# Three edits of order in an attention and non-local block: one activation behind a copy, four position groups in another order, and the last image's folded weights in two parts

## The chip, the cores and the metric

The kernel runs on one core of a Trainium2 chip. The metric is the device time of one execution in microseconds (us), the median of several runs. Every number is of 32-bit floating point work.

## The reference

The input is x, 8 images of 512 channels and 32 x 32 = 1024 positions. Two layers follow each other.

```python
# layer 0: attention with 8 heads of 64 channels, softmax over keys m
q, k, v = Wq x + bq, Wk x + bk, Wv x + bv          # 1x1 convolutions, 512 -> 512
out = softmax(q^T k / sqrt(64)) v
x = x + Wp out + bp
# layer 1: non-local block with 256 inner channels, then batch norm
g, theta, phi = g_w x + g_b, theta_w x + theta_b, phi_w x + phi_b
f = theta phi^T / 1024                             # 256 x 256 for each image
z = W_w (f g) + W_b + x
out = gamma (z - mean(z)) / sqrt(var(z) + eps) + beta   # over images and positions, by channel
```

The mean and the variance of a channel need z of all eight images, so no output can leave before the last image's z of that channel is there.

## The kernel before

**Work and order.** One image follows another: q, k, v, the attention of 16 units, the projection by Wp (`project`), theta and phi (`theta_phi`), and g, f and z (`nonlocal_`). The order of TensorE's matmuls and of VectorE's adds is pinned by hand: every instruction that goes through `pe()` or `dve()` keeps its place relative to the others that do, and a scheduler places the remaining ones around them. SyncE issues the loads and stores. ScalarE (ACT) makes the exponentials and copies results out of PSUM, VectorE (DVE) adds, and GpSimd (POOL) adds too.

**Products with fewer multiplications.** A product of two matrices is split into 2 x 2 quarters and made from seven products of sums of quarters in place of eight. `seven` does that for one product. `data` holds the quarters of x and their sums (`"11"`, `"21"`, `"22"`, `"t1"` to `"t4"`), and every product goes into the PSUM bank that `SEVEN` names for it. With positions_out the positions stand on the partitions of the result: a product then consists of four groups `parts` of 128 positions each, i = 0 to 3, where two of them fill half a bank. With `inner="tp"` (theta and phi of images 1 to 7, called ptp) some of the seven are again made from smaller products (`nested`), woven in between. The first product of ptp is `"11"`: its moving data are the folded weights w_tp, and its weights (the stationary operand) are columns of x, 128 positions at a time. These columns of x are finished only just before, by the last adds of the projection on DVE (L504, `add_to`, in place in x): two adds for columns 256 to 511, then two for columns 0 to 255.

`six` makes q, k and v of images 1 to 7 with seven products at each of two levels. `plain` makes product "11" in two halves: two matmuls each, then ACT writes the result with the bias into two places, the temporary T6 and quarter 11 (`begin`, the activation in L568). Then come three pairs of products of 14 steps each, in this order:

```python
    ORDER = "0a 0b 1a 2a 2b 1b 5a 4a 5b 4b 3a 3b 6a 6b".split()
```

The digit names the product, the letter the member of the pair. Products 0 and 2 of one member add up in the same bank, so 2b adds to what 0b left there. After a step its readers take the bank's content: the first reader of a quarter is an ACT copy (L479), the others are DVE adds (L481); the quarters T6 and 11 are only added to. The matmuls of these steps have line L473 for q and k. Sums of input quarters that later steps need are made on DVE or POOL in between (L294).

**The end.** Images 5, 6 and 7 (`LATE = 3`) get their z only when all else is done, since their f and g wait. `wf` is f folded into W and divided by 1024: two parts of 128 x 512 for each image, made by TensorE (pwf, L959) and scaled by ACT (L960). `late_unit` makes z of one image and channel chunk oc (128 channels) from wf and g: four matmuls into one bank (pz, L1038), each with two records in the profile, one DVE operation that adds bias and x (L1043), and two `bn_stats` (L1046). Image 5's z of chunk 0 stands ahead of image 7's wf, in `before_wf`. Then `last_z` runs:

```python
        order = [B - LATE, B - 1, *range(B - LATE + 1, B - 1)]
        for oc in range(CC):
            images = order if oc else [B - 1]
            for b in images:
                for h0, h1 in ((0, 1), (1, 2)) if b == images[-1] else ((0, NH),):
                    late_unit(b, oc, h0, h1)
            finish(oc, *begin(oc))
```

`begin` gathers the statistics into mean and variance (mv, L1062) and takes the square root on ACT (gs, L1064); `finish` makes scale and shift with three small DVE operations (L1070 to L1072), scales eight images (ACT L1079; in the last chunk half of them DVE L1077), and writes each one out from SyncE (L1080).

Of the kernel before, what the change touches and what calls it, by code (L numbers as in the profile page):

```python
# [30 lines left out]
def unshifted(ctx: ExitStack, tc: tile.TileContext, a: dict, out: bass.AP):  # L31
# [30 lines left out]
    def pe(ins):  # L62
        tc.keep_in_program_order(ins)
# [289 lines left out]
    def seven(name, w, data, positions_out, first, add, between=None, early=False,  # L353
              by_chunk=False, inner=None, via=()):

        nk, half = w.shape[2], w.shape[3]
        tags = list(free)
        free[:] = [tags[3], tags[1], tags[0], tags[2]] if early else [tags[3], tags[1], tags[2], tags[0]]  # L360
        slots, begun = {}, set()
        steps, counts = iter(()), iter(())
        if inner:
            free[:] = [tags[0], tags[2], tags[1], tags[3]] if inner == "p" else [tags[1], tags[2], tags[3], tags[0]]
            products, goes_to, counts = INNER[inner]
            counts = iter(counts)
            steps = nested(name, w, data, tags[2:], first, add, goes_to, positions_out)
        else:
            products = LATER if early == "later" else EARLY if early else SEVEN

        def read(reads, ps):
            for to, is_first in reads:
                (first if is_first else add)(to, ps)

        for n, (what, wi, di, s, reads) in enumerate(products):
            if s not in slots or early and what == "t4" or inner == "p" and what == "s3t3":
                slots[s] = bank(tags[s], f"{name}_{s}_{n}")
                begun -= {one for one in begun if one[0] == s}
            ps, d = slots[s], data[di]
            if positions_out:  # L380
                parts = [(ps.rearrange("p h (i f) -> p (h i) f", f=half)[:, i, :], i * half // 512,
                          lambda k, i=i: d[:, k, i * P:(i + 1) * P], lambda k: w[:, wi, k, :])
                         for i in range(512 // P)]
            else:
                parts = [(ps[:, m, :], m, lambda k, m=m: w[:, wi, k, m * P:(m + 1) * P], lambda k: d[:, k, :])
                         for m in range(half // P)]
            work = [(*part, k) for part in parts for k in range(nk)]
            if by_chunk and what in ("11", "s1t1"):
                work.sort(key=lambda one: one[4])
            for i, (to_ps, at, lhsT, rhs, k) in enumerate(work):  # L390
                pe(nc.tensor.matmul(to_ps, lhsT(k), rhs(k), start=(s, at) not in begun, stop=(k == nk - 1),  # L391
                                    skip_group_check=True))
                begun.add((s, at))
                for _ in range(next(counts, 0)):
                    next(steps)
            if inner and what in via:
                via[what](reads, ps)
            else:
                read(reads, ps)
            if between and n in between:  # L400
                between[n]()
# [4 lines left out]
    def six(name, w, data, positions_out, at, begin, third, fills, by_scalar=False, later=None):  # L406

        fills = dict(fills)
        shape = [P, 4, 256] if positions_out else [P, 2, 512]
        temps = {}  # L410

# [15 lines left out]
        def plain():  # L427
            d = data["11"]
            for half in range(2):
                ps = next_bank(f"{name}_0_{half}")[:, 0, :]  # L430
                if positions_out:
                    ps = ps.rearrange("p (i f) -> p i f", f=256)
                for i in range(2 if positions_out else 1):
                    for k in range(2):
                        if positions_out:
                            at = (half * 2 + i) * P
                            pe(nc.tensor.matmul(ps[:, i, :], d[:, k, at:at + P], w[:, 0, k, :],  # L437
                                                start=(k == 0 and i == 0), stop=(k == 1), skip_group_check=True))
                        else:
                            pe(nc.tensor.matmul(ps, w[:, 0, k, half * P:(half + 1) * P], d[:, k, :],  # L440
                                                start=(k == 0), stop=(k == 1), skip_group_check=True))
                for q in ("T6", "11"):
                    at_ = to(q)[:, half * 2:half * 2 + 2, :] if positions_out else to(q)[:, half, :]
                    begin(at_, ps, half)
            load_w("first")

        plain()
# [2 lines left out]
        for n, pair in enumerate(SIX):  # L450
            if n == 2:
                add("12", "22")
                add("12", "T6")
                for one in fills.pop("middle", ()):
                    one()
            slots = [next_bank(f"{name}_in_{n}_{i}") for i in range(4)]
            free[:] = [free[2], free[3], free[0], free[1]]
            begun = set()
            for step, which in enumerate(ORDER):
                _, wi, di, chain, reads = SEVEN[int(which[0])]  # L460
                m = "ab".index(which[1])
                outer, of, q = pair[m]
                a, d = w.inner(outer)[wi], data[f"inner {of}"][di]
                ps = slots[m if not chain else 2 + m][:, chain // 2, :256]
                start = (m, chain) not in begun
                begun.add((m, chain))
                if positions_out:
                    ps = ps.rearrange("p (i f) -> p i f", f=P)
                    for i in range(2):
                        pe(nc.tensor.matmul(ps[:, i, :], d[:, i * P:(i + 1) * P], a, start=start and not i, stop=True,  # L470
                                            skip_group_check=True))
                else:
                    pe(nc.tensor.matmul(ps, a, d, start=start, stop=True, skip_group_check=True))  # L473
                for (i, j), is_first in reads:
                    i, j = int(i) - 1, int(j) - 1
                    if is_first and q == "T7":
                        third(piece(q, i, j), ps, piece("T6", i, j), i)
                    elif is_first and q not in ("11", "T6"):
                        nc.scalar.copy(piece(q, i, j), ps)  # L479
                    else:  # L480
                        dve(nc.vector.tensor_tensor(piece(q, i, j), piece(q, i, j), ps, ALU.add))  # L481
                for one in fills.pop((n, step), ()):
                    one()
            load_w()
# [77 lines left out]
    def heads_of(b, what, w, bias, data, pin=lambda ins: None, steps=None, fills=None, **how):  # L562
# [2 lines left out]

        if fills is not None:
            def begin(to, ps, i):
                nc.scalar.activation(to, ps, AF.Identity, bias=bias[:, i:i + 1])  # L568

            def third(to, ps, of, i):  # L570
                if what == "q":
                    nc.scalar.activation(to, ps, AF.Identity, bias=steps[:, i:i + 1])
                else:
                    dve(nc.vector.scalar_tensor_tensor(to, ps, steps[:, i:i + 1], of, ALU.add, ALU.add))

            six(f"p{what}_{b}", w, data, False, lambda q: t[:, rows(q), cols(q)], begin, third, fills,
                what == "q", how.get("later"))
            return t
# [348 lines left out]
    def nonlocal_(b, xt, data, f, wg, before_wf, between=None, sums=None):  # L927
# [23 lines left out]
              between or {4: f_meanwhile}, early=bool(between))  # L951
        f = fs[0]

        before_wf()
        wf = block(f"wf_{b}")
        for d in range(IC):
            ps = next_bank(f"pwf_{b}_{d}")[:, 0, :]
            for c in range(IC):
# [90 lines left out]
            return sums  # L1049
        sums()  # L1050

    def last_z():
        order = [B - LATE, B - 1, *range(B - LATE + 1, B - 1)]
        for oc in range(CC):
            images = order if oc else [B - 1]
            for b in images:
                for h0, h1 in ((0, 1), (1, 2)) if b == images[-1] else ((0, NH),):
                    late_unit(b, oc, h0, h1)
            finish(oc, *begin(oc))

    def begin(oc):
# [51 lines left out]
    for b in range(B):  # L1113
# [137 lines left out]

        def before_wf():
            if last:
                late_unit(B - LATE, 0)
                z[b] = [xt[:, cc, :] for cc in range(CC)]
                reload(4, mats, "o")
                take_back(B - LATE + 1)
# [5 lines left out]
        if b == B - 2:  # L1263
            held.update(x=xt, both=both)
        else:
            nonlocal_(b, xt, data, None, weights("WgT"), before_wf, sums=both)
            load_w()
            if b in spill_g:
                put_away(b)
# [3 lines left out]
    dens, sane = both[:, 0, :], both[:, 1, :]  # L1273
    for to, d in own:
        nc.sync.dma_start(dens[:, to], d)
    last_z()


    good = const.tile([P, 1], F32, tag="good", name="good")
# [218 lines left out]
```

## Time and profile before

| | us |
|---|---|
| median of 3 runs | 2102.07 (2102.05 to 2102.19) |
| the profiled execution | 2102.2 |
| its span, first to last instruction | 2100.4 |
| TensorE busy in the span | 2076.9 (99%) |
| VectorE, ScalarE, GpSimd busy | 1442.6, 803.0, 818.3 |
| waits that ended last: TensorE's share of the chain | 98% |

The profile covers one execution; the 1.8 us between its time and its span lie ahead of the first and behind the last instruction. PE is the matmul stream of TensorE, and PEld its loading of stationary operands, which overlaps the matmuls. In a timeline each line has the start, the time to the end of the last record in the group, the engine, the line, the operation with output and inputs, and the number of records. A bracket gives the idle time of that engine just before, and what ended it. Each fp32 matmul appears twice, so four matmuls show as x8. Records of matmuls that follow each other closely overlap: their length is longer than the distance between two starts.

### The profile page before, as it was taken

What the parts mean: (1) busy time and instruction counts of PE and PEld (TensorE: products, weight loads), DVE (VectorE), ACT (ScalarE), POOL (GpSimd) and SP (SyncE); (2) the same over time, 40 slices, a digit from 0 to 9 for tenths busy, and PEclk for the clock granted to TensorE, in tenths of its full rate; (3) what the DMA queues carried; (4) which work ended last, traced back from release to release, by engine and by line L of the source; (5) the groups of instructions that cost most, each with busy time, mean ns of one, the idle gap of its engine ahead of it and who ended that gap; (6) DMA issues with size and microseconds to landing.
All of it is one profiled execution on the core that took longest, in us unless ns stands there. A gap on an engine that the chain in (4) does not pass through costs nothing.

```text
span 2100.4 us, 34471 instructions
## 1 busy us (share of the span) xinstructions
PE 2076.9 (99%) x13682; PEld 1176.0 (56%) x13682; DVE 1442.6 (69%) x2192; ACT 803.0 (38%) x1071; POOL 818.3 (39%) x689
## 2 busy tenths in 40 slices
PE   9999999999999999999999999999999999999995
PEld 4535864358733677336773377633876348743472
DVE  5587668775678656876567765677665775676756
ACT  1465204652046420564205641066312653056106
POOL 0024900448413583134922358223681338711010
PEclk9999999999999999999999999999999999999998
DMA  6254634445343443435324363153644345322668
GB/s 230 83 145 78 184 116 153 46 89 154 106 116 39 100 141 103 119 40 116 133 90 123 40 146 121 69 126 40 157 142 164 38 47 180 99 31 39 218 253 322
DMA packets 79697, 248.71 MB, mean 118 GB/s; under 512 B 17316, under 2 KB 25768, under 8 KB 77480
## 3 DMA queue, kind: packets, MB, share of 16 engines
q1 hardware_dynamic: 65656, 220.07, 32.3%
q0 software_dynamic: 12016, 24.80, 12.2%
q8 instruction: 110, 1.80, 0.4%
q10 hardware_dynamic: 1856, 1.56, 0.3%
q14 instruction: 59, 0.48, 0.1%
HBM read 164.64 MB, written 48.17 MB: 101 GB/s over the span
## 4 chain that ended last, share of the span: by engine, by line
PE 98%; ACT 1%; DVE 1%; DMA 0%; issue 0%
PE ps L638 21%; PE po L664 21%; PE ptp L391 7%; PE pv_in L470 6%; PE pp L391 6%; PE pk_in L473 6%; PE pq_in L473 6%; PE pg L391 5%; PE pz L391 3%; PE pp_in_s L342 3%; PE pf L916 2%; PE ptp_in_s L339 2%; PE pwf L959 1%; PE pv L437 1%; PE pq L440 1%; PE pq L391 1%
## 5 line engine op out<-in xcount | busy, mean ns | idle before, releaser
L641 ACT ACTIVATE e<-ps 128x1024 f32<-128x1024 f32 x512 | 523.0, 1025 | 412.0 <-PE ps L638 400.5
L694 POOL DMA_DIRECT2D fold<-acc x336 | 257.1, 816 | 921.7 <-DMA fold<-acc 543.3
L647 DVE TENSOR_TENSOR acc<-acc,e 128x1024 f32<-128x1024 f32 x384 | 469.9, 1224 | 93.2 <-ACT e L641 82.2
L638 PE MATMUL ps<-q,k 64*64 64x512 f32 x4096 | 529.2, 589 | 0.0
L664 PE MATMUL po<-e,v 64*64 64x512 f32 x4096 | 528.7, 589 | 0.0
L664 PEld LDWEIGHTS po<-e,v 64*64 64x64 f32 x4096 | 156.6, 133 | 282.9 <-issue 275.4
L638 PEld LDWEIGHTS ps<-q,k 64*64 64x64 f32 x4096 | 155.5, 133 | 283.2 <-issue 275.3
L947 ACT ACTIVATE g<-pg,gb 128x512 f32<-128x512 f32 x31 | 21.3, 688 | 366.5 <-PE pg L391 366.4
L645 DVE TENSOR_TENSOR acc<-e,e 128x1024 f32<-128x1024 f32 x64 | 78.3, 1224 | 114.5 <-ACT e L641 112.2
L391 PE MATMUL pp<-t_o,w_WpT 128*128 128x512 f32 x208 | 102.0, 592 | 0.0
L391 PE MATMUL ptp<-w_tp,t_x 128*128 128x256 f32 x400 | 96.1, 379 | 0.0
L756 POOL TENSOR_TENSOR o<-o,r 128x1024 f32<-128x1024 f32 x28 | 65.5, 2361 | 31.8 <-DMA r<-den_d 31.5
L391 PEld LDWEIGHTS ptp<-w_tp,t_x 128*128 128x128 f32 x400 | 72.3, 190 | 7.8
L821 POOL TENSOR_TENSOR x<-x,read 128x1024 f32<-128x1024 f32 x30 | 69.8, 2353 | 13.0 <-ACT read L818 13.0
L481 DVE TENSOR_TENSOR k<-k,pk_in 128x256 f32<-128x256 f32 x112 | 46.8, 421 | 39.5 <-PE pk_in L473 35.0
L391 PE MATMUL ptp<-w_tp,x 128*128 128x256 f32 x272 | 70.0, 381 | 0.8
L479 ACT COPY v<-pv_in 128x256 f32<-128x256 f32 x84 | 31.4, 374 | 95.0 <-DVE T_pv L481 25.5
L479 ACT COPY k<-pk_in 128x256 f32<-128x256 f32 x84 | 31.3, 372 | 92.0 <-PE pk_in L473 90.3
L481 DVE TENSOR_TENSOR v<-v,pv_in 128x256 f32<-128x256 f32 x112 | 46.3, 421 | 29.3 <-PE pv_in L470 22.8
L470 PE MATMUL pv_in<-w_WvT,i_t_x 128*128 128x128 f32 x448 | 59.2, 275 | 0.0
L473 PE MATMUL pk_in<-i_t_x,w_WkT 128*128 128x256 f32 x224 | 58.1, 381 | 0.1
L473 PE MATMUL pq_in<-i_t_x,w_WqT 128*128 128x256 f32 x224 | 57.5, 379 | 0.0
(250 smaller groups left out, 3249.6 us busy)
## 6 DMA issues: line engine op xcount, KB each, us to landing
fold<-acc POOLq DMA_DIRECT2D x336, 64.0 KB, 3.0
w_WqT<-kept_WqT SPq DMA_DIRECT2D x21, 896.0 KB, 5.8
w_WvT<-kept_WvT SPq DMA_DIRECT2D x21, 896.0 KB, 5.4
w_WkT<-kept_WkT SPq DMA_DIRECT2D x21, 896.0 KB, 6.6
r<-den_d SPq DMA_DIRECT2D x32, 512.0 KB, 6.8
x<-in_x_dram SPq DMA_DIRECT2D x30, 512.0 KB, 5.8
spill<-x SPq DMA_DIRECT2D x24, 512.0 KB, 4.0
z<-spill SPq DMA_DIRECT2D x24, 512.0 KB, 8.4
```

Of the source, the lines that this page charges most:

```text
L391: pe(nc.tensor.matmul(to_ps, lhsT(k), rhs(k), start=(s, at) not in begun, stop=(k == nk - 1), skip_group_check=True))
L470: pe(nc.tensor.matmul(ps[:, i, :], d[:, i * P:(i + 1) * P], a, start=start and not i, stop=True, skip_group_check=True))
L473: pe(nc.tensor.matmul(ps, a, d, start=start, stop=True, skip_group_check=True))
L481: dve(nc.vector.tensor_tensor(piece(q, i, j), piece(q, i, j), ps, ALU.add))
L638: pe(nc.tensor.matmul(ps[c * P // 2:(c + 1) * P // 2, j, :], k[r, p, keys], q[r, p, h * 512:(h + 1) * 512], start=True, stop=True, skip_gr ...
L641: nc.scalar.activation(e, ps, AF.Exp, scale=SCALE)
L645: nc.vector.tensor_tensor(accs[u], es[u, 0], e, ALU.add)
L647: ins = nc.vector.tensor_tensor(accs[u], accs[u], e, ALU.add)
L664: pe(nc.tensor.matmul(ps[j * D:(j + 1) * D, r, :], v[keys, m, (2 * p + j) * D:(2 * p + j + 1) * D], e[keys, j, :], start=(m == 0), stop=(m ...
L694: nc.gpsimd.dma_start(to, of, accum_op=ALU.add)
L756: dve((engine or nc.vector).tensor_tensor(at, at, of, ALU.mult))
L821: dve(nc.gpsimd.tensor_tensor(at, at, t, ALU.add))
```

## The change

It has three parts.

1. In `six`, for q and k: the activation that writes the second half of quarter 11 is not issued within `plain`, but after step 1 (product 0b), behind the ACT copy of that step. Both are pinned in that order.
2. In `seven` with `inner="tp"`: the product "11" makes its four position groups in the order 2, 3, 0, 1.
3. For image 7: the first 128 of 512 columns of wf are made ahead of `before_wf`, with one scaling for both parts of 128 rows. Image 5's z of chunk 0 follows, in halves. The other 384 columns are made in `last_z`, after image 7's z of chunk 0. In the other chunks the z of the last two images of `order` are made in halves, where before only the last was.

In the program, image 7's four pwf matmuls become eight narrower ones and VectorE gets four adds more (each of half the width); the instructions of ScalarE, GpSimd and SyncE keep their number.

```diff
@@ seven
             if positions_out:
                 parts = [(...)
-                         for i in range(512 // P)]
+                         for i in ((2, 3, 0, 1) if inner and what == "11" else range(512 // P))]
@@ six
         fills = dict(fills)
+        held_back = []
...
                 for q in ("T6", "11"):
                     at_ = to(q)[:, half * 2:half * 2 + 2, :] if positions_out else to(q)[:, half, :]
-                    begin(at_, ps, half)
+                    one = lambda at_=at_, ps=ps, half=half: dve(begin(at_, ps, half))
+                    if half and q == "11" and not positions_out:
+                        held_back.append(one)
+                    else:
+                        begin(at_, ps, half)
...
                     elif is_first and q not in ("11", "T6"):
-                        nc.scalar.copy(piece(q, i, j), ps)
+                        ins = nc.scalar.copy(piece(q, i, j), ps)
+                        if held_back:
+                            dve(ins)
                     else:
                         dve(nc.vector.tensor_tensor(piece(q, i, j), piece(q, i, j), ps, ALU.add))
+                if step == 1 and held_back:
+                    held_back.pop()()
@@ nonlocal_
-        before_wf()
         wf = block(f"wf_{b}")
+
+        def some_wf(at):
+            ps = next_bank(f"pwf_{b}_{at.start}")[:, :, at]
+            for d in range(IC):
+                for c in range(IC):
+                    pe(nc.tensor.matmul(ps[:, d, :], f[:, c, d * P:(d + 1) * P], ww[:, c, at], start=(c == 0),
+                                        stop=(c == IC - 1)))
+            nc.scalar.mul(wf[:, :, at], ps, 1.0 / N)
+
+        if b == B - 1:
+            some_wf(slice(0, P))
+            before_wf()
+            late[b] = xt, g, [wf[:, d, :] for d in range(IC)]
+            return lambda: some_wf(slice(P, C))
+        before_wf()
         for d in range(IC):
@@ last_z
-                for h0, h1 in ((0, 1), (1, 2)) if b == images[-1] else ((0, NH),):
+                for h0, h1 in ((0, 1), (1, 2)) if b in images[-2:] else ((0, NH),):
                     late_unit(b, oc, h0, h1)
+            if oc == 0:
+                rest_of_wf()
             finish(oc, *begin(oc))
@@ before_wf
             if last:
-                late_unit(B - LATE, 0)
+                for h in range(NH):
+                    late_unit(B - LATE, 0, h, h + 1)
```

More of the change, by code (lines that the diff above doesn't have):

```diff
@@ L567, in begin @@
             def begin(to, ps, i):
-                nc.scalar.activation(to, ps, AF.Identity, bias=bias[:, i:i + 1])
+                return nc.scalar.activation(to, ps, AF.Identity, bias=bias[:, i:i + 1])
             def third(to, ps, of, i):
@@ L952, in nonlocal_ @@
         f = fs[0]
+        wf = block(f"wf_{b}")
+        def some_wf(at):
[10 more added lines that the diff above has]
+            return lambda: some_wf(slice(P, C))
         before_wf()
-        wf = block(f"wf_{b}")
         for d in range(IC):
@@ L1050, in late_unit, with last_z @@
         sums()
-    def last_z():
+    def last_z(rest_of_wf):
         order = [B - LATE, B - 1, *range(B - LATE + 1, B - 1)]
@@ L1265, in unshifted @@
         else:
-            nonlocal_(b, xt, data, None, weights("WgT"), before_wf, sums=both)
+            rest_of_wf = nonlocal_(b, xt, data, None, weights("WgT"), before_wf, sums=both)
             load_w()
@@ L1275, in unshifted @@
         nc.sync.dma_start(dens[:, to], d)
-    last_z()
+    last_z(rest_of_wf)
     good = const.tile([P, 1], F32, tag="good", name="good")
```

## The prediction

> **What bounds the kernel now.** I read the page's head first, then its chain of waits, then the waits by line and tile, and then the timeline, engine by engine, at each place that the change touches.
>
> ```profile
> span 2100.4 us, 34471 instructions
> PE 2076.9 (99%) x13682; PEld 1176.0 (56%) x13682; DVE 1442.6 (69%) x2192; ACT 803.0 (38%) x1071; POOL 818.3 (39%) x689
> ...
> PE 98%; ACT 1%; DVE 1%; DMA 0%; issue 0%
> ```
>
> TensorE (PE) is the bound: busy for 2076.9 of 2100.4 us and 98% of the chain. An edit off PE saves only what PE waits for it. A busy PE also hides short stalls, since a stalled matmul's record overlaps its neighbours, so the stalls must be read from starts. A 128x256 record follows the one before after 0.215 us (two at 533.07, the next two at 533.50).
>
> First place, the q product of image 1, step 2b. The PE timeline, the weight loads and ACT:
>
> ```profile
> 450.68 1.40 PE L473 MATMUL pq_in<-i_x,w_WqT 128*128 128x256 f32 x5
> ...
> 451.60 0.30 PEld L473 LDWEIGHTS pq_in<-i_x,w_WqT 128*128 128x128 f32 x2 [0.29 <-ACT q L479]
> ...
> 450.02 0.69 ACT L568 ACTIVATE T_pq<-pq,bq 128x512 f32<-128x512 f32 x1 [0.45 <-PE pq L440]
> 450.60 0.68 ACT L568 ACTIVATE q<-pq,bq 128x512 f32<-128x512 f32 x1
> 451.17 0.37 ACT L479 COPY q<-pq_in 128x256 f32<-128x256 f32 x1
> ...
>   ACT q L479: 2.1, 7
>   ACT k L479: 2.1, 7
> ```
>
> Five records should take 4 x 0.215 + 0.38 = 1.24 us; they take 1.40, so PE loses 0.16 us. The weight load after 450.68 + 3 x 0.215 = 451.33 starts 0.27 late, behind the copy: 0.11 of its lateness costs nothing. The copy itself waits in line on ACT behind two activations. The last two lines (waits of the weight loads of L473: us, times) say that it happens 14 times, once in each q and k of images 1 to 7: 14 x 0.162 = 2.27 us.
>
> Second place, the start of theta-phi in image 1:
>
> ```profile
> 535.23 0.59 PE L342 MATMUL pp_in_s<-i_o,w_WpT 128*128 128x256 f32 x2
> 535.95 3.69 PE L391 MATMUL ptp<-w_tp,x 128*128 128x256 f32 x16
> ...
> 533.71 0.85 DVE L504 TENSOR_TENSOR x<-x,pp_in_s 128x256 f32<-128x256 f32 x2 [0.87 <-PE pp_in_s L342]
> 535.43 0.85 DVE L504 TENSOR_TENSOR x<-x,pp_in_s 128x256 f32<-128x256 f32 x2 [0.87 <-PE pp_in_s L342]
> ...
> 535.92 1.16 PEld L391 LDWEIGHTS ptp<-w_tp,x 128*128 128x128 f32 x6 [0.50 <-issue]
> ```
>
> The first ptp record should start at 535.23 + 2 x 0.215 = 535.66 and starts at 535.95: 0.29 lost. Its weight load waits for the first DVE add of 535.43, which ends near 535.85. The load of the next chunk waits for the second add, another 0.08 us. The five later images show the same gap (792.84 to 793.56, 1050.11 to 1050.83 and on); image 7 does not, as its projection ends otherwise. So 6 x 0.37 = 2.22 us.
>
> Third place, the tail after 2049 us (output issues on SP, chain lines on ACT and DVE, and stretches with DMA share and GB/s last):
>
> ```profile
> 2059.31 1.46 SPq L1080 DMA_DIRECT2D out_dram<-x  x2
> 2062.56 6.69 SPq L1080 DMA_DIRECT2D out_dram<-z  x7
> ...
> 2060.74 0.29 ACT L1064 ACTIVATE gs<-mv,eps 128x1 f32<-128x1 f32 x1 [0.33 <-DVE mv L1062]
> ...
> 2054.73 1.28 DVE L1043 SCALAR_TENSOR_TENSOR x<-pz,Wb,x 128x1024 f32<-128x1024 f32 x1 [0.83 <-PE pz L1038]
> ...
> 2049.00:2055.00 6.00, 6.00 (x16) 2.65 (x15) 4.47 (x10) 4.32 (x6) 0.00 (x0) 1.00 0.32 126
> 2055.00:2065.00 10.00, 10.00 (x25) 4.50 (x24) 8.81 (x15) 8.99 (x10) 0.00 (x0) 1.00 1.00 397
> 2075.00:2085.00 10.00, 3.72 (x9) 1.33 (x7) 9.15 (x16) 9.32 (x10) 0.00 (x0) 0.94 1.02 405
> ```
>
> From 2055 the output stream fills the DMA engines. At 405 GB/s a 512 KB piece takes 1.29 us and the eight of one channel chunk (oc) 10.4 us; the issues of oc 1 and oc 2 start 10.37 us apart. PE (12 x 0.858 = 10.3 us for one oc) and ACT go at the same pace. One seam is left: oc 1's first issue, 2.1 us after the last one of oc 0, waits for its mean and variance (mv).
>
> [...]
>
> **The change part by part.**
>
> *A, the held activation (14 stages).* Nothing is added; one 0.68 us activation goes behind a 0.37 us copy. The copy can start when the activation ahead of it lets it, at about 450.60, but product 0b ends only near 450.84, so it runs about 450.9 to 451.25, and the load due at 451.33 is in time. Gain: 0.162. New wait: the held activation now ends near 451.83 instead of 451.28. Two things are queued behind it. Step 1b rewrites what it has read: about 0.125 late, 0.02 lost. The DVE add of 1a, in line on DVE with the adds and input sums behind it (L481, L294), ends near 452.29; step 5a's load waits for that, about 0.155 late, 0.05 lost. For k the same sum gives the same. The trace of before cannot show this wait. Bounds: none of it costs PE (2.27 us gained in all) or it eats the whole gain (0). I take 0.162 - 0.05 = 0.112, times 14: **-1.57 us**.
>
> *B, group order 2, 3, 0, 1 (images 1 to 7).* No instruction is added. The first two groups read columns 256 to 511, which the adds of 533.71 finished at 534.56, 0.9 us before the load is due. Groups 0 and 1 come 8 records, 1.7 us, later (537.4), and their adds end at 536.28. What is late next: the second product needs a DVE sum released at 538.78, and its load is due at 538.90; that just holds. If it doesn't, at most 0.1 us a time comes back. **-6 x 0.37 = -2.22 us**; image 7 gives nothing.
>
> *C, image 7's folded weights first, and D, z in halves.* The eight 128x512 pwf records (3.43 us) become 8 of 128 columns (estimated from the pitch: 0.86) and 8 of 384 (2.57): no PE time added. pz of image 5 then covers the first ACT scaling (256 wide, 0.37 as the copy's row). Image 7's first z, at 2044.13 before, comes 2.57 earlier, and with it mv and gs of oc 0. The rest of the scaling (768 wide, between the rows of 0.60 for 512 and 1.03 for 1024: some 0.85 with its wait) stands on ACT behind that gs, so the first output issue comes 2.2 to 2.3 us earlier, from 2051.81. The DVE adds in halves: 2 x 0.73 for 1.28, with the statistics interleaved some 0.33 more for an oc, but the 0.83 us wait goes; mv of oc 1 is then 0.42 to 0.52 earlier, held by PE's last half of image 6. The SP issues keep their number and order.
>
> Of the 2.2 us nothing reaches the end by itself: oc 0's transfers would be done by about 2061.4, the stream then runs dry, and oc 1's first issue moves only with its mv. From there ACT and DMA run without a break. Bounds: 0, if oc 1's gain is lost on the last pieces, and -2.5, if oc 1 followed oc 0. I take **-0.45 us**.
>
> Sum: -1.57 - 2.22 - 0.45 = -4.24 us. The profiled execution took 2102.2 us (its span and 1.8 around it): 2102.2 - 4.24 = 2097.96. The median lies 0.13 lower, so the forecast is 2102.07 - 4.24 = **2097.8 us**.
>
> **The rivals.**
>
> 1. *The new wait eats A.* For: DVE takes the adds in line, and 5a comes only a few records after 1a. Against: the load has 0.11 us that cost nothing. It gives -2.67: 2099.4.
>
> 2. *A whole and more in the tail.* With no cost at 5a, -2.27 - 2.22 - 0.45 = -4.94 (2097.1). With the tail's -1 to -1.5 besides, as when the last pieces' uneven landing shortens too: 2096.0 to 2096.6. For: the last two pieces took 1.5 and 2.8 us to land where the others took 1.3. Against: nothing in the change spreads them better.
>
> 3. *The tail's whole 2.5 us.* That is right if the outputs of oc 0 held up oc 1. It gives 2095.8. Against: the seam at 2062.56.
>
> 4. *Slower.* The held activation delays DVE's queue at 1a in all 14 stages, and through the sums in that queue also the next products. From 0.162 us lost a stage (a load 0.27 late) A as a whole is a loss; to end 0.2% slower against B and the tail, each stage must lose 0.162 + (4.2 + 2.7) / 14 = 0.65 us, which is a load 0.76 late; I compute 0.155. At 0.75 us lost, 2102.07 - 2.67 + 14 x 0.59 = 2107.6.
>
> 5. *It does not do what it says.* If the first weight load of theta-phi waits for another write of the same buffer than the adds I named, B gives nothing: 2102.07 - 1.57 - 0.45 = 2100.0.
>
> **How the numbers follow.** A measurement of this kernel tells about 0.2%, 4.2 us, from no change; the sum lies right on that line. Forecast 0.50 (2097.0 to 2098.7 by A's and C's own bounds), about two thirds of it beyond the line, 0.32, since B and A's direction are read off and one more stall of 0.4 us, in the k of image 3 at 765, which I left out, may go too. Rivals 2 and 3 together 0.26, faster. Rival 1 0.14 and rival 5 0.04, the same. Rival 4 0.06. Faster 0.32 + 0.26 = 0.58, same 0.18 + 0.14 + 0.04 = 0.36, slower 0.06. The range for 8 in 10 goes from 2096.2 (rival 2's tail) to 2099.6 (rival 1 whole).
>
> **What would show it.** A: in the waits of L473's weight loads the two lines of 2.1 us are gone; on ACT the copy (L484 now) starts near 450.9 less what was gained before; any price stands as a DVE wait at 5a or an ACT wait at 1b. B: ptp starts 0.215 us after the last pp_in_s record. C and D: the first output issue about 2.2 us earlier than its stage, a dip in DMA share between oc 0 and oc 1, the 0.83 wait gone. A pair of product stages that still take 0.16 more than back to back would prove A wrong; a shift of all of oc 1's issues by over 1 us, C.

## The result and the profile after

The changed kernel takes 2098.24 us (median of 17 runs, 2097.66 to 2098.90) against 2102.29 us before (17 runs, 2102.03 to 2103.27): 4.05 us less, a ratio of 0.998 with a 95% interval of 0.9973 to 0.9986. The forecast was 2097.8. The prediction named 4.2 us as what a measurement tells from no change, and gave 0.58 to a gain beyond that line: 4.05 us lies just inside that line, though the interval does not reach 1. The profiled span went from 2100.4 to 2096.3 us.

The head of the page and its chain of waits:

```profile
span 2096.3 us, 34491 instructions
PE 2074.2 (99%) x13690; PEld 1177.0 (56%) x13690; DVE 1446.7 (69%) x2196; ACT 804.6 (38%) x1071; POOL 818.7 (39%) x689
...
PE 98%; ACT 1%; DVE 0%; DMA 0%; issue 0%; DVEq 0%
```

TensorE is still the bound, and the head shows little of where 4 us went. For that the places are read again. Step 2b of image 1's q, in the PEld timeline, then ACT's:

```profile
450.60 1.27 PEld L478 LDWEIGHTS pq_in<-i_x,w_WqT 128*128 128x128 f32 x6
452.02 0.30 PEld L478 LDWEIGHTS pq_in<-i_x,w_WqT 128*128 128x128 f32 x2 [0.16 <-ACT q L577]
452.48 0.30 PEld L478 LDWEIGHTS pq_in<-x,w_WqT 128*128 128x128 f32 x2 [0.16 <-DVE q L488]
```

```profile
450.15 0.69 ACT L577 ACTIVATE T_pq<-pq,bq 128x512 f32<-128x512 f32 x1 [0.45 <-PE pq L441]
451.01 0.37 ACT L484 COPY q<-pq_in 128x256 f32<-128x256 f32 x1 [0.18 <-PE pq_in L478]
451.28 0.69 ACT L577 ACTIVATE q<-pq,bq 128x512 f32<-128x512 f32 x1
```

The six loads that begin at 450.60 now run through: 2b's is among them, without a wait. ACT waits for TensorE's product 0b and copies at once. (All of this is some 0.1 us later than the prediction's times, since this execution started later; see the table.) The held activation runs behind the copy, and two shorter waits have appeared. The waits of these weight loads, summed over the kernel:

```profile
  ACT q L577: 1.1, 7
  ACT k L577: 1.1, 7
  DVE k L488: 1.1, 7
  DVE q L488: 1.1, 7
```

Each is 0.16 us, 7 times for q and 7 for k, where before there was one of 0.29. The start of theta-phi (PE timeline):

```profile
535.13 0.59 PE L342 MATMUL pp_in_s<-i_o,w_WpT 128*128 128x256 f32 x2
535.57 1.67 PE L391 MATMUL ptp<-w_tp,x 128*128 128x256 f32 x7
```

From 535.13 to 535.57 are two records of 0.215 us and no gap. The tail, first ACT, then the output issues on SP (the first line of the kernel before, the others of the changed one), one DVE line, then stretches with TensorE's clock, DMA share and GB/s in the last three columns:

```profile
2043.96 0.29 ACT L1089 ACTIVATE gs<-mv,eps 128x1 f32<-128x1 f32 x1 [7.32 <-DVE mv L1087]
2044.40 0.81 ACT L971 ACTIVATE wf<-pwf 128x768 f32<-128x768 f32 x1
2045.10 7.16 ACT L1104 ACTIVATE z<-z,shift,gs 128x512 f32<-128x512 f32 x7
2052.17 2.36 ACT L1104 ACTIVATE x<-x,shift,gs 128x1024 f32<-128x1024 f32 x2
2056.84 0.29 ACT L1089 ACTIVATE gs<-mv,eps 128x1 f32<-128x1 f32 x1 [2.30 <-DVE mv L1087]
```

```profile
2051.81 6.70 SPq L1080 DMA_DIRECT2D out_dram<-z  x7
...
2045.93 6.70 SPq L1105 DMA_DIRECT2D out_dram<-z  x7
2053.43 1.47 SPq L1105 DMA_DIRECT2D out_dram<-x  x2
2058.64 6.70 SPq L1105 DMA_DIRECT2D out_dram<-z  x7
...
2050.35 0.73 DVE L1066 SCALAR_TENSOR_TENSOR x<-pz,Wb,x 128x512 f32<-128x512 f32 x1
```

```profile
2049.00:2055.00 6.00, 6.00 (x16) 2.65 (x15) 5.74 (x10) 5.53 (x5) 0.00 (x0) 1.00 1.01 406
2056.00:2058.00 2.00, 2.00 (x6) 0.83 (x5) 1.47 (x6) 0.49 (x2) 0.00 (x0) 1.00 0.99 395
2058.00:2060.00 2.00, 2.00 (x6) 0.88 (x5) 1.78 (x2) 2.00 (x3) 0.00 (x0) 1.00 0.25 98
2060.00:2062.00 2.00, 2.00 (x6) 0.95 (x5) 1.97 (x4) 2.00 (x3) 0.00 (x0) 1.00 0.77 307
```

The first output of chunk 0 now leaves at 2045.93 (before 2051.81), so the output stream is full from 2049 on. But ACT then idles 2.30 us for the mean and variance of chunk 1, and the stream falls to 98 GB/s. The DVE add for image 7's z of chunk 1, which waited 0.83 us before, starts without a wait.

Where the 4.1 us of span went, from the starts of the matmul records (the time between two starts less the 0.2145 us that 256 columns take, where it is more than a few ns) and the output issues:

| | lost or at, before | after | difference |
|---|---|---|---|
| q and k steps, lost | 3.00 | 1.43 | -1.57 |
| start of theta-phi, lost | 2.22 | 0 | -2.22 |
| k of image 0, TensorE at | 29.00 | 29.29 | +0.29 |
| a stall in image 0's projection, lost | 0 | 0.07 | +0.07 |
| end of image 7's g, TensorE at | 2037.26 | 2033.86 | -3.40 |
| first output of chunk 0 at | 2051.81 | 2045.93 | -5.88 |
| first output of chunk 1 at | 2062.56 | 2058.64 | -3.92 |
| first output of chunk 3 at | 2083.24 | 2079.27 | -3.97 |

The first four rows add up to -3.43, against -3.40 at the end of g. From there to chunk 3 the tail gives -0.57 (3.97 - 3.40), and the span ends 0.1 us sooner behind chunk 3's first output than before. Why the k of image 0 begins later is taken up with the sum below.

### The profile page after: what moved, and what is told of

Read it like the earlier page. It is cut to its first block, busy times and chain, and to the rows that moved or that the text cites. A ratio compares the mean times of both kernels' runs of the same rounds, so it can differ in the third digit from the quotient of the medians.

```text
span 2096.3 us, 34491 instructions
## 1 busy us (share of the span) xinstructions
PE 2074.2 (99%) x13690; PEld 1177.0 (56%) x13690; DVE 1446.7 (69%) x2196; ACT 804.6 (38%) x1071; POOL 818.7 (39%) x689
## 4 chain that ended last, share of the span: by engine, by line
PE 98%; ACT 1%; DVE 0%; DMA 0%; issue 0%; DVEq 0%
PE ps L647 21%; PE po L673 21%; PE ptp L391 7%; PE pv_in L475 6%; PE pp L391 6%; PE pk_in L478 6%; PE pq_in L478 6%; PE pg L391 5%; PE pz L391 3%; PE pp_in_s L342 3%; PE pf L925 2%; PE ptp_in_s L339 2%; PE pv L438 1%; PE pq L441 1%; PE pq L391 1%; PE pv L391 1%
```

## The experiments

Each of the first runs takes one part of the change by itself: A (the held activation), B (the group order), C and D (the tail). All times are medians, and each run's difference is taken to the kernel before as timed beside it: 2102.55 for the three parts and the first run with T6, 2102.68 for C, for D, for the doubled activation and for three parts of the weights, and 2102.69 for the last three runs.

**One part at a time.** *Held activation alone:*

```diff
 # the kernel before with part 1 of the change; its first lines
...
+                    if half and q == "11" and not positions_out:
+                        held_back.append(one)
```

> Only the held activation (the edit in six). Theory: 14 stages lose 0.05 us each to the two new waits instead of 0.162, so about 1.57 us less than before, 2100.7 against 2102.3; the weight loads of the q and k steps show waits on the activation and on DVE of 0.16 us each, and none of 0.29 on the copy. Rival (the new wait takes the whole gain): no change, 2102.3, with over 0.15 us lost at step 5a. Rival (A recovered in full): 2100.0.

Measured: 2101.06, 1.49 less (ratio 0.9992, 0.9984 to 1.0001). The interval touches no change, so the trace has to decide: the q and k steps lose 1.42 us instead of 3.00, and their four waits are those of the changed kernel, none on the copy. The span fell by only 0.4, since the profiled execution, the slowest of the 13, lost time elsewhere: the k of image 0 begins 0.73 us later (29.72 against 29.00), and another 0.45 us goes in image 0's projection, where TensorE waits for DVE's adds into x; these stand behind a weight sum on DVE that took 2.82 us in place of 1.19 (2.44 in the changed kernel's profile).

*Group order alone:*

```diff
-                         for i in range(512 // P)]
+                         for i in ((2, 3, 0, 1) if inner and what == "11" else range(512 // P))]
```

> Only the order 2, 3, 0, 1 of the position groups in theta-phi. Theory: the 0.37 us ahead of theta-phi go in six images, 2.22 us less than before, 2100.1; theta-phi starts 0.43 us after the last pair of projection records began, and nothing else moves. Rival (another write of x is waited for, or the second product becomes late): under 1 us less, over 2101.3, with a new gap within the first three products.

Measured: 2100.20, 2.35 less (0.9989, 0.9983 to 0.9996). The PE timeline of image 1:

```profile
535.33 0.59 PE L342 MATMUL pp_in_s<-i_o,w_WpT 128*128 128x256 f32 x2
535.76 1.46 PE L391 MATMUL ptp<-w_tp,x 128*128 128x256 f32 x6
```

The distance is 0.43, six times. No gap came in its place; the q and k steps lose 2.98 us, as before. For the weight load at 535.92 the profile of before named no releaser; that it waited for the adds was read from the times, and this run bears it out.

*The last image's part alone (parts of the change 1 and 2 left out):*

> Only the last image's part: first quarter of the folded weights ahead, image 5's first z and image 7's z in halves. Theory: the first output is issued about 2.5 us earlier than before, the first of channel chunk 1 about 0.5 earlier, and the end moves with the latter: 0.4 to 0.6 us less, 2101.7. Rival (the output stream as a whole moves with its first piece): 2.5 us less, 2099.8.

Measured: 2101.92, 0.63 less (0.9997, 0.9988 to 1.0005). First outputs of chunks 0, 1 and 3 at 2049.45, 2062.16 and 2082.78: 2.36, 0.40 and 0.46 earlier than before, in an execution that lost 0.11 more at the start. The three parts' differences add up to 4.47; the whole change gave 4.05 in its first runs and 4.30 in a later series (below). Runs of one kernel spread by about 1 us.

**Which half of the tail carries it.** *C without D (the edit as against the run before):*

```diff
-                for h0, h1 in ((0, 1), (1, 2)) if b in images[-2:] else ((0, NH),):
+                for h0, h1 in ((0, 1), (1, 2)) if b == images[-1] else ((0, NH),):
```

> Only part C: the first quarter of the folded weights ahead, image 5's first z behind it and in halves; image 7's z of chunks 1 to 3 stays whole. Theory (the seam between chunk 0 and chunk 1 swallows what chunk 0 gains): the first output is issued about 2.5 us earlier than before, but the first of chunk 1 not (0 to 0.1), and the time is that of before, 2102.5. Rival (the end follows the first output): 2.5 us less, 2100.

*D without C (the same line the other way, on the kernel before):*

> Only part D: image 7's z of chunks 1 to 3 in halves. Theory: the 0.83 us wait of DVE in chunk 1 goes, the mean and variance of chunk 1 are 0.4 to 0.5 us earlier, and the time is 0.4 to 0.5 us less than before, 2102.1, nearly all of what C and D give together. Rival (C carries the gain, or both are needed): no change, 2102.5, since ACT and the output stream of chunk 0 are in the way.

The issues on SP, C alone and then D alone:

```profile
2049.24 6.76 SPq L1096 DMA_DIRECT2D out_dram<-z  x7
2056.73 1.77 SPq L1096 DMA_DIRECT2D out_dram<-x  x2
2062.41 1.04 SPq L1096 DMA_DIRECT2D out_dram<-z  x2
```

```profile
2051.88 6.70 SPq L1080 DMA_DIRECT2D out_dram<-z  x7
2059.38 1.46 SPq L1080 DMA_DIRECT2D out_dram<-x  x2
2062.19 1.04 SPq L1080 DMA_DIRECT2D out_dram<-z  x2
```

C alone: chunk 0 leaves 2.57 us earlier, chunk 1 0.15 (0.10 of it because this execution was ahead by that much from the start), and the time is 2102.60, 0.08 less (ratio 1.0, 0.9992 to 1.0009). D alone: chunk 0 does not move (2051.88), chunk 1 leaves 0.37 earlier (in an execution 0.06 behind from the start), and the time is 2102.20, 0.48 less (0.9998, 0.9989 to 1.0006). Both times lie within the spread; the issue times tell them apart. What chunk 0 gains is swallowed by the wait for chunk 1, and D by itself brings the tail's gain, as far as these runs tell.

**What the held activation costs.** *A known dose more: the activation issued twice in a row, with the same values.*

```diff
                 if step == 1 and held_back:
-                    held_back.pop()()
+                    one = held_back.pop()
+                    one()
+                    one()
```

> The changed kernel, with the held activation issued twice in a row, writing the same values: the slower-side rival in a known dose. It ends some 0.58 us later (distance of two activations). Theory (the stall is the lateness less 0.1 us, handed from ACT by the bank to step 1b, and over the DVE add of 1a to 5a): 1b and 5a together lose about 0.6 us a stage more, 14 x 0.58 = 8.1 us more than the changed kernel, 2106.4, slower than before. Rival (DVE and PE have room for a late activation): under 3 us more, 2101 at most.

Measured: 2108.78, slower than before (1.0028, 1.0018 to 1.0039) and 10.4 us over the changed kernel's 2098.39 (its second series, below). ACT, then the weight loads:

```profile
453.02 0.37 ACT L484 COPY q<-pq_in 128x256 f32<-128x256 f32 x1 [0.18 <-PE pq_in L478]
453.29 1.41 ACT L579 ACTIVATE q<-pq,bq 128x512 f32<-128x512 f32 x2
```

```profile
454.75 0.30 PEld L478 LDWEIGHTS pq_in<-i_x,w_WqT 128*128 128x128 f32 x2 [0.88 <-ACT q L579]
455.21 0.30 PEld L478 LDWEIGHTS pq_in<-x,w_WqT 128*128 128x128 f32 x2 [0.16 <-DVE q L488]
```

The two activations have the same destination and start 1.41 - 0.69 = 0.72 us apart, not 0.58 as two that write to different places (450.02 and 450.60 before): in the trace the first takes 0.687 us, and the second begins 33 ns after that has ended. The wait at 1b went from 0.16 to 0.88, by just that, and the steps of q and k lose 11.5 us instead of 1.43: 10.1 us more, 0.72 a stage. So the delay reaches 1b as the theory said (a wait of 0.88 us; the trace names the activation, not the bank), and its dose was too small. The wait at 5a stayed at 0.16: 1b stops TensorE first, and 5a moves back with it.

*The other activation held: the one of T6, needed only in the next pair.*

```diff
-                    if half and q == "11" and not positions_out:
+                    if half and q == "T6" and not positions_out:
```

> The changed kernel, but the activation that is held back is the one that writes half 1 of T6, which is not needed until the next pair, instead of half 1 of quarter 11, to which product 1a is added at once. Theory (the DVE add of 1a waits for the held activation and hands the delay to 5a): the 0.16 us wait on DVE goes in 14 stages, the one on ACT at step 1b stays, and PE loses 0.025 us instead of 0.05 a stage: 0.35 us less than the changed kernel, about 2097.9. Rival (5a waits for something else, as the bank or ACT): the same waits and the same time as the changed kernel, 2098.2.

Measured: 2097.81 (0.9978, 0.9969 to 0.9986). The weight loads:

```profile
452.41 0.30 PEld L478 LDWEIGHTS pq_in<-i_x,w_WqT 128*128 128x128 f32 x2 [0.16 <-ACT T_pq L577]
452.73 0.41 PEld L478 LDWEIGHTS pq_in<-x,w_WqT 128*128 128x128 f32 x2
```

The wait on DVE ahead of 5a is gone, the one on ACT stays, and the q and k steps lose 1.06 us instead of 1.43. That shows the road: activation, DVE add of 1a, load of 5a. To compare the times, both kernels were timed once more, side by side.

> The changed kernel once more, beside the two others of this call on the same chip: 2098.2. The lost time in the q and k steps is 0.05 us a stage as before; the first loads' arrival may shift the start by some tenths of a us.

> The variant with T6 held once more, beside the changed kernel on the same chip. Theory: 0.35 us less than the changed kernel. Rival: the difference seen between the calls was the start's noise, and nothing is left.

Measured: 2098.39 for the changed kernel, 2097.86 with T6 held, 0.53 less; 0.43 less in the first pair of medians, which were not taken side by side. The direction came twice and the trace has 0.37 us of it, but the two ratios to before (0.998, 0.9971 to 0.9988; 0.9977, 0.9968 to 0.9985) overlap.

**Can the seam between chunks be closed?** *Folded weights in three parts, on the variant with T6 held:*

```diff
-            return lambda: some_wf(slice(P, C))
+            return lambda: some_wf(slice(P, 2 * P)), lambda: some_wf(slice(2 * P, C))
...
-            if oc == 0:
-                rest_of_wf()
+            if oc < len(rest_of_wf):
+                rest_of_wf[oc]()
```

> A candidate: the changed kernel with T6 held instead of quarter 11, and the folded weights in three parts: columns 0 to 127 as in the change, 128 to 255 after image 7's z of chunk 0, the other 256 after the z of chunk 1. Theory (the first output of chunk 1 waits for its z, whose matmuls stand behind 2.57 us of folded weights): 1.72 us of matmuls leave their place ahead of chunk 1, its mean and variance and the end come 1.2 to 1.7 us earlier: about 2096.3 against 2097.8 with T6 alone. Rival (ACT or the output stream is the bound from chunk 0 on): 2097.8, with the first output of chunk 1 early but the last where it was.

*In four parts of 128 columns:*

> As the candidate with three parts and T6 held, but the folded weights in four parts of 128 columns, each just behind the z of the chunk before. Theory (with three parts the matmuls that left chunk 1 came back ahead of chunk 2, whose first output stayed at 2069.1): 0.86 us of them now move on to chunk 3, so the first output of chunk 2 comes up to 0.86 us earlier, and that of chunk 3 up to 0.6, where TensorE's last matmul, which cannot move, takes over. 0.3 to 0.6 us less than with T6 alone. Rival (TensorE's last matmul decides already, or the last pieces of the output): no gain.

Measured: 2098.28 (0.9978, 0.9969 to 0.9987) and 2098.12 (0.9977, 0.9968 to 0.9986), both against 2097.81 and 2097.86 with T6 alone: no gain. First issues of chunks 1, 2 and 3 on SP with T6 alone, in three and in four parts:

```profile
2058.74 6.70 SPq L1105 DMA_DIRECT2D out_dram<-z  x7
...
2069.05 6.70 SPq L1105 DMA_DIRECT2D out_dram<-z  x7
...
2079.36 5.99 SPq L1105 DMA_DIRECT2D out_dram<-z  x6
```

```profile
2057.13 6.70 SPq L1105 DMA_DIRECT2D out_dram<-z  x7
...
2069.08 6.70 SPq L1105 DMA_DIRECT2D out_dram<-z  x7
...
2079.39 6.03 SPq L1105 DMA_DIRECT2D out_dram<-z  x6
```

```profile
2057.00 6.69 SPq L1105 DMA_DIRECT2D out_dram<-z  x7
...
2068.19 6.70 SPq L1105 DMA_DIRECT2D out_dram<-z  x7
...
2079.39 5.37 SPq L1105 DMA_DIRECT2D out_dram<-z  x6
```

Three parts move chunk 1 by 1.6 us and chunk 2 not at all; four move chunk 2 by 0.9 and chunk 3 not at all. The seam wanders to where the last folded weights are made. In four parts ACT waits for the mean and variance of chunk 3, where with T6 alone it went on without a wait:

```profile
2077.57 0.29 ACT L1089 ACTIVATE gs<-mv,eps 128x1 f32<-128x1 f32 x1 [0.78 <-DVE mv L1087]
```

The mean and variance of chunk 3 need TensorE's last z, and the sum of TensorE's work is the same in all three. The rival of that expectation was right; which half of it is not settled. In four parts even the last piece is issued 0.63 us sooner than with T6 alone (2086.09 against 2086.72) and the span does not end sooner (2096.5 against 2096.4), so the landing of the last pieces may hold the end as well.

## Why the prediction was right, and where a term was off

- **The bound** was read rightly: the gain came from TensorE's short stalls, which the busy share doesn't show, and was found by starts.
- **A**: forecast -1.57; the q and k steps lost 1.57 us less, and the run of A alone took 1.49 less. The two new waits at 1b and 5a came where they were said to be. The working named a loss of 0.02 at 1b and of 0.05 at 5a and took 0.05 for both; added up, the two would have made it 0.07 and A -1.29. Measured was 0.025 at each, so the 0.05 that was taken came true, with another split. Rival 1 fell (0.025 us lost at 5a, not 0.16), and so did the whole recovery of rival 2: the price was there.
- **B**: forecast -2.22, measured -2.22 in the trace and 2.35 in time. The second product did not become late. Rival 5 fell.
- **C and D**: forecast -0.45. The trace has -0.57 up to chunk 3's first output; alone they gave 0.63. The step "nothing of the 2.2 us reaches the end by itself" held: C alone gave 0.08. Off was the term for the rest of the scaling on ACT: I put 0.3 us on its way to the first output (2.57 down to 2.2 to 2.3), but most of its 0.81 us ran while DVE made scale and shift. From gs to the first scaling ACT took 1.14 us in place of 0.97, so it cost 0.17, and the first output came 2.48 us earlier than its stage. For the end the miss did not matter, as chunk 1 decides. Rival 3 fell with it.
- **The sum** was -4.24 and -4.05 was measured. That they lie so close is in part luck, since two misses went opposite ways. In the trace the three terms gave -4.36 (1.57, 2.22 and 0.57), and what the sum did not have took 0.36 back: 0.07 in image 0's projection and 0.29 at the start.
- **The start.** The first records of image 0's q start 0.854 and 0.613 us apart in the changed kernel, without a wait for another engine or a transfer, and then 0.429. The warm-up matmuls ahead of them (128 columns) are 0.213 apart, and only the last two in the run of C alone 0.111. So TensorE goes at half its pace at first in these profiles, though their clock column shows 1.00 there, and this stretch ends sooner in one execution than in another (by the distances at 4.2 and 5.9 us). It costs image 0's q 0 to 0.43 us in the five profiles without A and 0.61 to 1.23 in the eight with it; in some a wait for a load of Wq comes on top (TensorE idle for 0.17 us in the run of C alone). Two executions of the changed kernel begin the k of image 0 at 29.29 and at 30.02. The times speak against A as the cause: the profiled executions of the four runs without A lie below their kernels' medians (that of C alone is the fastest of 13), while six of the eight with A lie above (that of A alone is the slowest of 13), so the profiles differ in which execution was caught. What ends the slow stretch was not tried.
- **Rival 4** was priced about rightly: 2107.6 for 0.75 us lost a stage; the run with the activation twice lost 0.77 and took 2108.78, on a baseline 0.6 higher than the 2102.07 of that working. The changed kernel was far from it, with a wait of 0.16 where the copy's had been 0.29.
- The stall of 0.4 us in the k of image 3, which might have gone, is still there (0.30 and 0.10 us). The weight load waits there 0.54 us for a DVE step on T_pk; that step's cause was not tried.

## What to carry to other kernels

When one engine is 99% busy, look for its stalls in the distances between starts, and then for what the late releaser stood behind in its own queue: moving a result that nobody needs soon behind one that is needed at once costs no instruction. Of two results that could be held, hold the one whose next reader is farthest away (here 0.37 us more in the trace). And before making the first piece of an output stream earlier, find what the second piece waits for: here a 2.5 us gain went into that seam, and closing the seam only moved it to a later chunk, and the end stayed where it was.

## What the runs showed of the hardware

In the q and k steps a weight load's wait cost the matmuls 0.13 us less than it lasted: waits of 0.29 us (before), 0.16 (the changed kernel) and 0.88 (the activation twice) cost 0.16, 0.025 and 0.75. Two ACT activations of 128x512 that write to different places started 0.58 us apart (450.02 and 450.60 before); where both had the same destination (the activation twice) the second started 0.72 us after the first, which took 0.687. TensorE started at half its pace: 512 columns took 0.854 us a record and later 0.429 in the changed kernel's profile, and by these distances the change comes about 4.2 us after the first instruction in one execution (C alone, from the warm-up matmuls) and 5.9 us after it in another (the changed kernel).
